# A selective scan in four layers: units of 128 channels by one state against units of 64 channels by two

## The chip, the core and the metric

The kernel runs on one core of a Trainium2 chip. Times are device microseconds (us) of that core. In the profile PE is the matrix engine (PEld its weight loads), DVE is VectorE, ACT is ScalarE, POOL is GpSimd, and SP is the engine whose queue issues all the transfers (DMAs) here. L804 is line 804 of the kernel before.

## The reference, cut to what matters

Four layers of a two-dimensional state space model (SS2D) run one after the other on an image batch of 8 x 48 x 48 with 96 channels. In each layer the input is projected to 192 inner channels and convolved to u; then, for K = 4 directions (rows, columns, and both reversed), there is a scan over the L = 2304 positions, with N = 16 states per channel:

```python
delta = jax.nn.softplus(dts + dt_projs_bias.reshape(K, Din)[None, :, :, None])
def step(h, inp):
    u, dl, Bv, Cv = inp
    dA = jnp.exp(dl[..., None] * A)
    h = h * dA + (dl * u)[..., None] * Bv[:, :, None, :]
    y = jnp.einsum('bkdn,bkn->bkd', h, Cv)
    return (h, y)
```

For each channel, state and position there is one exponential, one product with B, one step of the scan, one product with C, and a sum over the 16 states. Afterwards the directions are added, normalised, gated and projected back.

## The kernel before, in words

The image batch is taken in pairs of images. The 2 x 192 channels of a pair fill three tiles of 128 partitions: t = 0 and 1 hold the first 128 channels of each image, t = 2 the last 64 of both. For each layer, pair, tile and direction (ph for rows or columns, d for forward or reversed) the positions are cut into three chunks of 768. A unit is one chunk and one state n: 128 channels by 768 positions. Layers 0 to 2 have 3 x 4 x 12 x 3 = 432 chunks and 6912 units. Layer 3 works on short pieces at the ends of the image (the class Edge), four states to a unit.

A unit goes through the engines like this:

- SP loads the row C of state n, broadcast to 128 partitions, into a tile cb (`load`, L715), three units ahead (LOADS).
- ScalarE makes da = exp(A delta) (`exp`, L726), two or three units ahead (DECAYS).
- PE spreads the row B over 128 partitions by a product with a matrix of zeros and ones, into the PSUM tile b (`spread`, L743), one unit ahead. There are two such tiles.
- VectorE multiplies b by delta u (`scan`, L755) and scans (L759).
- GpSimd multiplies cb by the result (L768).
- PE adds cb into acc, by a product with the identity, four units later (`add_up`, L804, LAG = 4). After a chunk's sixteenth sum ScalarE copies acc into y (`collect`, L819); there is one acc, so the first sum of the next chunk (L798, which also brings in the y so far) waits for that copy.

Each fourth unit (n = 3, 7, 11, 15, `pooled`) differs in layers 0 to 2: B comes by a transfer into a tile bb (`load_b`, L687), GpSimd multiplies it by delta u (`weigh`, L698), and ScalarE's exponential goes to PSUM, into one of the two tiles b.

For the next chunk, `prepare` makes delta (c.dl) and delta u (c.du) beside the units, in two halves of 384 positions: a projection on PE (L585), softplus on ScalarE and GpSimd, its last step on VectorE (L607), a copy to c.dl on ScalarE (L609), and the product with u on VectorE (L611 or L614). The loop in `run` takes one step of it per unit. It begins at n = 0 and must be through at n = 13, when the first exponential of the next chunk is issued. Beside the units, the previous pair's epilogue and the next pair's prologue also go on in small steps.

The order of each engine is the program's order (`keep_order`), so what stands ahead in an engine's queue must be done first, its waits included. The loop issues per unit, in this order: loads, the spread, GpSimd's B, exponentials (`get_ready`), copies of the carries, the products and scan, then the sum of four units ago and one step each of `prepare` and of the side work.

Of the kernel before, what the change touches and what calls it, by code (L numbers as in the profile page):

```python
# [63 lines left out]
QUAD = 4  # L64

# [37 lines left out]
def ss2d_layers_kernel(ctx: ExitStack, tc: tile.TileContext, x_in, consts, weights, out):  # L103
# [10 lines left out]
    bbpool = ctx.enter_context(tc.tile_pool(name="bb", bufs=3))  # L114
    apool = ctx.enter_context(tc.tile_pool(name="da", bufs=5))
# [34 lines left out]
    pick = cpool.tile([NR, NS], BF16, name="pick")  # L150
    pick2 = cpool.tile([2 * NR, NS, P], BF16, name="pick2")
    sel = cpool.tile([P, 2, NS], F32, name="sel")
    for b in range(2):
        nc.vector.tensor_reduce(
            sel[:, b, :],
            ident[:, NR * b : NR * b + NR].rearrange("p (k n) -> p n k", k=PARTS),
            mybir.AxisListType.X,
            ALU.add,
        )
        nc.vector.tensor_copy(  # L160
            pick2[:, :, 64 * b : 64 * b + 64],
            sel[: 2 * NR, b, :].unsqueeze(2).to_broadcast([2 * NR, NS, 64]),
        )
    nc.vector.tensor_copy(pick, sel[:NR, 0, :])
# [21 lines left out]
    class Layer:  # L186
# [17 lines left out]
        def derive(self):  # L204
# [11 lines left out]
            nc.scalar.activation(self.a, self.a, AF.Copy, scale=-1.0)  # L216
            yield
# [335 lines left out]
    def load_dt(c):  # L553
        r = layers[c.l].rank
        c.dts = sm2.tile([64, SCAN], F32, name="dts", tag="dts")
# [6 lines left out]

    def prepare(c):
# [3 lines left out]
        c.dl = ddpool.tile([P, SCAN], F32, name="dl", tag="dl")[:, : c.m]  # L567
        c.du = ddpool.tile([P, SCAN], F32, name="du", tag="du")[:, : c.m]
# [6 lines left out]
        for z in range(0, c.m, HALF):  # L575
# [33 lines left out]
            nc.scalar.copy(c.dl[:, at], v)  # L609
            if ph == 0:  # L610
                nc.vector.tensor_mul(c.du[:, at], v, u[:, c.c0 + z : c.c0 + z + m])  # L611
            else:
                r0 = (c.c0 + z) // H
                nc.vector.tensor_mul(  # L614
                    c.du[:, at].rearrange("p (w h) -> p w h", h=H),
# [3 lines left out]
            if z + m == c.m and l == NLAYER - 1:  # L619
                c.sum_up()  # L620
            if z + m == c.m:
                yield
# [6 lines left out]
    def columns_of(l, t, ph, d, n):  # L629
        k = ph + 2 * d  # L630
        return layers[l].a[:, int(t == 2), k * NS + n : k * NS + n + 1]

    def picked(t, n):

        if t == 2:
            return 2 * NR, pick2[:, n, :]
        return NR, pick[:, n : n + 1].to_broadcast([NR, P])

# [13 lines left out]
    class Chunk:  # L652


        def __init__(self, l, p, t, ph, d, i, group, turned):
# [6 lines left out]
            self.brow = self.acc = self.dts = None  # L662
            self.cb, self.da, self.rq, self.b = {}, {}, {}, {}

        def sum_up(self):

            f = self.dl if self.d == 0 else self.dl[:, ::-1]
            nc.vector.tensor_tensor_scan(
                f, ones.to_broadcast([P, self.m]), f,
                0.0 if self.first else self.group["sum"], ALU.mult, ALU.add,  # L670
            )
            self.group["sum"] = z = capool.tile([P, 1], F32, name="sum", tag="sum")
            nc.scalar.copy(z, f[:, self.m - 1 : self.m])
# [4 lines left out]

        def load_b(self, n):
            if not self.pooled(n):  # L680
                return
            s, m, at = state[self.l, self.p], self.m, slice(self.c0, self.c0 + self.m)
            row = 2 * layers[self.l].rank + 2 * NS * self.d + n
            self.b[n] = b = bbpool.tile([P, SCAN], F32, name="bb", tag="bb")
            for z in self.batches:
                o = b[64 * z : 64 * z + 64] if self.t == 2 else b
                nc.sync.dma_start(  # L687
                    o[:, :m],
                    s["xd"][self.ph, z, row : row + 1, at].to_broadcast(
                        [64 if self.t == 2 else P, m]  # L690
                    ),
                )

        def weigh(self, n):

            if self.pooled(n):
                b = self.b[n][:, : self.m]
                nc.gpsimd.tensor_mul(b, b, self.du)  # L698

        def load(self, n):  # L700

            s, m, at = state[self.l, self.p], self.m, slice(self.c0, self.c0 + self.m)
            if n == 0:
                self.brow = rpool.tile([2 * NR, SCAN], BF16, name="brow", tag="brow")
                for j, b in enumerate(self.batches):
# [4 lines left out]
            row = 2 * layers[self.l].rank + 2 * NS * self.d + NS + n  # L710
            self.cb[n] = cb = cbpool.tile([P, SCAN], F32, name="cb", tag="cb")
            for b in self.batches:
                o = cb[64 * b : 64 * b + 64] if self.t == 2 else cb
                rows = s["xd"][self.ph, b, row : row + 1, at]
                nc.sync.dma_start(  # L715
                    o[:, :m], rows.to_broadcast([64 if self.t == 2 else P, m])
                )
# [6 lines left out]
        def exp(self, n, da):  # L724
            self.da[n] = da = da[:, : self.m]
            nc.scalar.activation(  # L726
                da, self.dl, AF.Exp, scale=columns_of(self.l, self.t, self.ph, self.d, n)
            )

        def spread(self, n):  # L730
# [9 lines left out]
            k, w = picked(self.t, n)  # L740
            self.b[n] = b = pb.tile([P, 2 * BANK], F32, name="b", tag="b")
            for z, zm in pieces(self.m):
                nc.tensor.matmul(  # L743
                    b[:, z : z + zm], w, self.brow[:k, z : z + zm], start=True, stop=True
                )

        def scan(self, n):
# [6 lines left out]
            if not self.pooled(n):  # L754
                nc.vector.tensor_mul(b, self.du, b)  # L755
# [30 lines left out]
        def add_up(self, n):  # L786
# [3 lines left out]
            elif n == 0:  # L790
# [6 lines left out]
                for a in range(2):  # L797
                    nc.tensor.matmul(  # L798
                        self.acc[:, a, : self.m // 2], w, self.y_part(z)[:, a],
                        start=True, stop=False,  # L800
                    )
            c = self.halves(self.cb.pop(n)[:, : self.m])
            for a in range(2):
# [527 lines left out]
```

## Time and profile before

The median of three runs is 21131.63 us (21129.68 to 21134.72).

| what | value |
|---|---|
| profiled execution, span | 21129.7 us |
| PE, sums (L804) | 27648 records, 10706.0 us busy |
| PE, spreads (L743) | 10368 records |
| DVE, scans (L759) | 6912, mean 1736 to 1814 ns |
| DVE, products (L755) | 5184, mean 948 ns |
| ACT, exponentials (L726) | 6912, mean 903 to 926 ns |
| POOL, products (L768) | 6912, mean 1813 ns |
| all transfers | 3832.96 MB, 61.9% of the queues' time |
| mean granted clock of PE | 0.951 |

A matrix product in 32-bit floats shows as two records. A busy engine is one that has a record running; the ends of PE's records are modelled, so a busy PE needn't be at its peak. The times of groups overlap between engines and aren't to be added up. A wait is named by the instruction that came late and by the one that released it.

### The profile page before, as it was taken

The page shows a single profiled execution, that of the slowest core. Times are in us where ns is not written, and L with a number is a line of the kernel's source. Part 1 is how long each engine was busy: PE and PEld are TensorE (multiplying, and loading weights), DVE is VectorE, ACT ScalarE, POOL GpSimd, SP SyncE. Part 2 cuts the span into 40 slices and gives each one's busy share as a digit, 9 for nine tenths or more (in the row PEclk, how much of TensorE's full clock was granted, in tenths as well). Part 3 has the DMA queues.
Part 4 walks back from the last instruction along what each step waited for, and adds up shares of the span by engine and source line. Part 5 has one row for each costly group of instructions (what it writes and reads, how often), then busy time and mean ns, then how long its engine had stood idle before and what let it go on. Part 6 is the DMA issues. An engine that isn't in the chain of part 4 may idle for free. (4 is left out here: it accounts for less than half of the span.)

```text
span 21129.7 us, 229163 instructions
## 1 busy us (share of the span) xinstructions
PE 18566.6 (88%) x64610; PEld 9118.1 (43%) x64610; DVE 18834.4 (89%) x15938; ACT 13520.6 (64%) x23969; POOL 17984.5 (85%) x11081
## 2 busy tenths in 40 slices
PE   8988998998998998998998988998998998988886
PEld 3333444443444443443443443443443443444555
DVE  6999999999999999999999999999999999997453
ACT  5555666666666665665666666665665666667776
POOL 5999898898899899898899989898999899896442
PEclk8999999999999999999999999999999999999887
DMA  4666666676676676676676666666666666674221
GB/s 137 195 193 193 188 196 194 190 196 195 190 200 195 192 201 195 190 204 191 191 204 195 191 194 195 190 197 190 191 197 193 190 196 195 189 194 123 79 74 51
DMA packets 1707632, 3832.96 MB, mean 181 GB/s; under 512 B 238448, under 2 KB 575216, under 8 KB 1693168
## 3 DMA queue, kind: packets, MB, share of 16 engines
q1 hardware_dynamic: 1706352, 3818.21, 61.9%
q8 instruction: 521, 8.54, 0.2%
q14 instruction: 759, 6.22, 0.1%
HBM read 3665.08 MB, written 152.27 MB: 181 GB/s over the span
## 5 line engine op out<-in xcount | busy, mean ns | idle before, releaser
L804 PE MATMUL acc<-cb,cst 128*128 128x384 f32 x27648 | 10706.0, 516 | 0.0
L768 POOL TENSOR_TENSOR cb<-cb,da 128x768 f32<-128x768 f32 x5184 | 9349.5, 1813 | 1393.2 <-DVE da L759 875.6
L804 PEld LDWEIGHTS acc<-cb,cst 128*128 128x128 f32 x27648 | 5003.6, 196 | 3957.4 <-issue 1498.2
L759 DVE TENSOR_TENSOR_SCAN da<-da,carry,b 128x768 f32<-128x768 f32 x3456 | 6268.3, 1814 | 220.9 <-ACT b L726 3.7
L755 DVE TENSOR_TENSOR b<-du,b 128x768 f32<-128x768 f32 x5184 | 4912.0, 948 | 685.4 <-PE b L743 678.8
L726 ACT ACTIVATE da<-dl,a 128x768 f32<-128x768 f32 x5184 | 4770.4, 926 | 95.6 <-POOL cb L768 60.4
L743 PE MATMUL b<-brow,pick 48*128 48x512 bf16 (+3 forms) x10368 | 2652.0, 337 | 1581.8 <-DVE da L759 1239.4
L726 ACT ACTIVATE b<-dl,a 128x768 f32<-128x768 f32 x1728 | 1560.3, 903 | 2960.1 <-DVE da L759 2817.4
L698 POOL TENSOR_TENSOR bb<-bb,du 128x768 f32<-128x768 f32 x1728 | 3131.3, 1812 | 183.4 <-DMA bb<-xd 142.8
L768 POOL TENSOR_TENSOR cb<-cb,bb 128x768 f32<-128x768 f32 x1728 | 3134.0, 1814 | 161.5 <-issue 56.8
L759 DVE TENSOR_TENSOR_SCAN da<-da,b 128x768 f32<-128x768 f32 x1728 | 3030.5, 1754 | 110.2 <-ACT b L726 2.4
L743 PEld LDWEIGHTS <-pick 48*128 48x128 bf16 (+1 forms) x10368 | 669.2, 97 | 4379.9 <-DVE da L759 2363.1
L759 DVE TENSOR_TENSOR_SCAN bb<-b,carry,bb 128x768 f32<-128x768 f32 x1152 | 2069.3, 1796 | 5.9 <-ACT b L726 2.2
L301 PE MATMUL ps<-pad,diag 128*128 128x480 f32 (+1 forms) x4320 | 2015.0, 565 | 15.1 <-DVE du L611 9.6
L650 ACT COPY carry<-da 128x1 f32<-128x1 f32 x3456 | 627.1, 181 | 1086.3 <-DVE da L759 1076.4
L590 ACT ACTIVATE ps<-ps,w 128x384 f32<-128x384 f32 (+1 forms) x912 | 497.1, 545 | 1027.5 <-PE ps L585 1022.9
L301 PEld LDWEIGHTS ps<-pad,diag 128*128 128x128 f32 x4320 | 804.2, 193 | 725.2 <-issue 330.3
L603 POOL TENSOR_TENSOR lg<-lg,w 128x384 f32<-128x384 f32 (+1 forms) x912 | 892.4, 978 | 195.0 <-ACT w L601 194.8
L585 PE MATMUL ps<-dts,w 6*128 6x384 f32 (+5 forms) x2432 | 821.2, 523 | 240.6 <-DVE du L611 99.9
L759 DVE TENSOR_TENSOR_SCAN bb<-b,bb 128x768 f32<-128x768 f32 x576 | 1000.1, 1736 | 16.3 <-POOL bb L698 9.8
L604 POOL TENSOR_TENSOR lg<-lg,e 128x384 f32<-128x384 f32 (+1 forms) x912 | 889.5, 975 | 71.2
L798 PE MATMUL acc<-y,cst 128*128 128x384 f32 x1008 | 619.1, 745 | 192.2 <-ACT y L819 127.2
(141 smaller groups left out, 17243.9 us busy)
## 6 DMA issues: line engine op xcount, KB each, us to landing
cb<-xd SPq DMA_DIRECT2D x4736, 384.0 KB
cb<-xd SPq DMA_DIRECT2D x4736, 192.0 KB
bb<-xd SPq DMA_DIRECT2D x1152, 384.0 KB
bb<-xd SPq DMA_DIRECT2D x1152, 192.0 KB
yd<-y SPq DMA_DIRECT2D x48, 1152.0 KB
ey<-yd SPq DMA_DIRECT2D x256, 216.0 KB
brow<-xb SPq DMA_DIRECT2D x576, 72.0 KB
ex<-xs SPq DMA_DIRECT2D x256, 108.0 KB
```

The source lines that it names most:

```text
L301: nc.tensor.matmul(ps[:, :m], ly.diag[:, int(t == 2), j, :], pad[:, r0 + dy : r0 + dy + nr, dx : dx + W], start=(j == 0), stop=(j == 8),)
L585: nc.tensor.matmul(o[:, :m], ly.dtw[q0 : q0 + r, k, chans], dts[q0 : q0 + r, at], start=True, stop=True,)
L603: nc.gpsimd.tensor_sub(lg, lg, w1)
L604: nc.gpsimd.tensor_add(lg, lg, e)
L650: nc.scalar.copy(*late_act.pop(0))
L698: nc.gpsimd.tensor_mul(b, b, self.du)
L726: nc.scalar.activation(da, self.dl, AF.Exp, scale=columns_of(self.l, self.t, self.ph, self.d, n))
L743: nc.tensor.matmul(b[:, z : z + zm], w, self.brow[:k, z : z + zm], start=True, stop=True)
L755: nc.vector.tensor_mul(b, self.du, b)
L759: nc.vector.tensor_tensor_scan(way(h), way(da), way(b), start, ALU.mult, ALU.add)
L768: nc.gpsimd.tensor_mul(c, c, h)
L804: nc.tensor.matmul(self.acc[:, a, : self.m // 2], ident, c[:, a, :], start=False, stop=(n == NS - 1 and not self.turns),)
```

## The change

A unit becomes 64 channels by two states. Unit n works on half g = n % 2 of the tile's channels, and on states n // 2 and n // 2 + 8: the first in partitions 0 to 63, the second in 64 to 127. Therefore delta and delta u have to stand in both halves of the partitions, once for each g. ScalarE copies each half to its own place, and a transfer on SP's queue, SBUF to SBUF, makes the twin (`to_twins`). The rates A are rearranged the same way (`a2`). The rows of B and C are fetched or spread per 64 partitions.

The sum over states now has to add the two halves of the partitions as well: PE multiplies by two identities of 64 stacked on each other (`twin`), which gives 64 rows of output, and it does so for both g, into the two halves of acc. Those are two tiles of 64 columns of the array. A sum takes two units at once, at odd n, and LAG is 3.

`prepare` begins one unit earlier, right after the last scan of a chunk, and what must be through at n = 13 is delta alone (`ready`); delta u may follow until the chunk ends. In the buffers, delta and delta u double, and bb goes from 3 to 2, da from 5 to 4, dts from 2 to 1. The core of the diff:

```diff
-    bbpool = ctx.enter_context(tc.tile_pool(name="bb", bufs=3))
-    apool = ctx.enter_context(tc.tile_pool(name="da", bufs=5))
+    bbpool = ctx.enter_context(tc.tile_pool(name="bb", bufs=2))
+    apool = ctx.enter_context(tc.tile_pool(name="da", bufs=4))
...
+    pick = cpool.tile([2 * NR, 2, NS], BF16, name="pick")
...
+    twin = cpool.tile([P, 64], F32, name="twin")
+    nc.vector.tensor_add(twin, ident[:, 0:64], ident[:, 64:P])
...
-        c.dts = sm2.tile([64, SCAN], F32, name="dts", tag="dts")
+        c.dts = sm1.tile([64, SCAN], F32, name="dts", tag="dts")
...
+    def to_twins(z, at):
+
+        nc.sync.dma_start(z[64:P, 0, at], z[0:64, 0, at])
+        nc.sync.dma_start(z[0:64, 1, at], z[64:P, 1, at])
+
     def prepare(c):
...
-        c.dl = ddpool.tile([P, SCAN], F32, name="dl", tag="dl")[:, : c.m]
-        c.du = ddpool.tile([P, SCAN], F32, name="du", tag="du")[:, : c.m]
+        dl = ddpool.tile([P, 2, SCAN], F32, name="dl", tag="dl")[:, :, : c.m]
+        du = ddpool.tile([P, 2, SCAN], F32, name="du", tag="du")[:, :, : c.m]
+        c.dl, c.du = ([z[:, 0], z[:, 1]] for z in (dl, du))
...
             nc.vector.scalar_tensor_tensor(v, v, 0.0, lg, ALU.max, ALU.add)
             yield
-            nc.scalar.copy(c.dl[:, at], v)
-            if ph == 0:
-                nc.vector.tensor_mul(c.du[:, at], v, u[:, c.c0 + z : c.c0 + z + m])
...
+            for g in range(2):
+                nc.scalar.copy(dl[64 * g : 64 * g + 64, g, at], v[64 * g : 64 * g + 64])
+            to_twins(dl, at)
             if z + m == c.m:
-                yield
+                if l == NLAYER - 1:
+                    c.sum_up()
+                c.ready = True
+            yield
+            times_u(v)
+            yield
+            for g in range(2):
+                nc.scalar.copy(du[64 * g : 64 * g + 64, g, at], v[64 * g : 64 * g + 64])
+            to_twins(du, at)
...
+    def spread_rows(o, rows, batches, states):
+
+        for h, (b, n) in enumerate(zip(batches, states)):
+            nc.tensor.matmul(
+                o[64 * h : 64 * h + 64], pick[:, b, n : n + 1].to_broadcast([2 * NR, 64]), rows,
+                start=True, stop=True,
+            )
...
+        def states(self, n):
+            return n // 2, n // 2 + PAIRED
+
+        def fetch(self, o, first, n):
+
+            xd = state[self.l, self.p]["xd"]
+            b = n % 2 if self.t == 2 else self.t
+            for h, i in enumerate(self.states(n)):
+                row = 2 * layers[self.l].rank + 2 * NS * self.d + first + i
+                nc.sync.dma_start(
+                    o[64 * h : 64 * h + 64, : self.m],
+                    xd[self.ph, b, row : row + 1, self.c0 : self.c0 + self.m].to_broadcast(
+                        [64, self.m]
+                    ),
+                )
...
-                da, self.dl, AF.Exp, scale=columns_of(self.l, self.t, self.ph, self.d, n)
+                da, self.dl[n % 2], AF.Exp,
+                scale=layers[self.l].a2[:, int(self.t == 2), n % 2, k, i : i + 1],
...
-                nc.vector.tensor_mul(b, self.du, b)
+                nc.vector.tensor_mul(b, self.du[n % 2], b)
...
+            if n % 2 == 0:
+                return
+            c = [self.halves(self.cb.pop(i)[:, : self.m]) for i in (n - 1, n)]
+            for a in range(2):
+                for g in range(2):
                     nc.tensor.matmul(
-                        self.acc[:, a, : self.m // 2], w, self.y_part(z)[:, a],
-                        start=True, stop=False,
+                        self.acc[64 * g : 64 * g + 64, a, : self.m // 2], twin, c[g][:, a, :],
+                        start=False, stop=(n == NS - 1 and not self.turns),
                     )
-            c = self.halves(self.cb.pop(n)[:, : self.m])
-            for a in range(2):
-                nc.tensor.matmul(
-                    self.acc[:, a, : self.m // 2], ident, c[:, a, :],
-                    start=False, stop=(n == NS - 1 and not self.turns),
-                )
...
-    LAG = 4
+    LAG = 3
...
-            if n == 0:
-                drain(coming)
...
+            if k == 0:
+                coming_to = 1
+                coming = prepare(chunks[coming_to])
             if n == max(0, per - 1 - DECAYS):
-                drain(coming)
+                while coming_to < len(chunks) and not chunks[coming_to].ready:
+                    next(coming)
...
             c.scan(n)
+            if n == per - 1:
+                drain(coming)
...
+                coming_to = chunks.index(c) + 2
+                coming = prepare(chunks[coming_to]) if coming_to < len(chunks) else iter(())
```

## The prediction

> **What bounds the kernel now.** I read the busy shares first, then VectorE's waits, then the order of time inside one chunk of 16 units.
>
> From the page, part 1:
>
> ```profile
> PE 18566.6 (88%) x64610; PEld 9118.1 (43%) x64610; DVE 18834.4 (89%) x15938; ACT 13520.6 (64%) x23969; POOL 17984.5 (85%) x11081
> ```
>
> Three engines look almost full. PE is the least so: its ends are modelled, and in the timeline four records of L804 in a row take 1.56 us and eight 2.85, so one adds 0.32. By that the 27,648 records of L804 fill about 8.9 ms, not 10.7. VectorE's rows are honest: 6912 units of a scan of 1.8 us, and 5184 products of 0.95 us, are 17.3 ms. Stretch by stretch VectorE is 93 to 95% busy from 0.5 to 19 ms (layers 0 to 2) and half idle in layer 3. So VectorE sets the time of layers 0 to 2, and a faster PE is worth only what VectorE waits for PE. The table of waits says how much (waiter, releaser: total us, times, longest):
>
> ```profile
> PE b L743 <- DVE da L759: 1239.4, 959, 5.2
> DVE b L755 <- PE b L743: 678.8, 619, 6.2
> PEld acc L798 <- ACT y L819: 241.7, 248, 4.1
> ```
>
> 679 us is the whole prize, 3.2%. The third line is one cause: the first sum of a chunk waits for the copy of the last one, and the broadcasts behind it on PE are late. The clock is another. Two stretches of 10 us (PE, PEld, DVE, ACT, POOL busy, granted clock, DMA share, GB/s):
>
> ```profile
> 5028.00:5038.00 10.00, 7.71 (x26) 3.40 (x24) 9.82 (x10) 8.62 (x21) 8.63 (x7) 1.00 0.75 216
> 5050.00:5060.00 10.00, 10.00 (x16) 4.17 (x16) 7.71 (x6) 7.48 (x11) 6.08 (x5) 0.50 0.40 111
> ```
>
> At half clock PE is full and VectorE falls to 77%.
>
> Now the end of a chunk without carries (unit 12 ends at 4950.40; the rows are the products and scans of units 13, 14, 15 and 16, then ScalarE's exponentials of 15, 17 and on):
>
> ```profile
> 4950.77 0.95 DVE L755 TENSOR_TENSOR b<-du,b 128x768 f32<-128x768 f32 x1
> 4951.75 1.81 DVE L759 TENSOR_TENSOR_SCAN da<-da,carry,b 128x768 f32<-128x768 f32 x1
> 4953.48 0.94 DVE L755 TENSOR_TENSOR b<-du,b 128x768 f32<-128x768 f32 x1
> ...
> 4956.19 1.79 DVE L759 TENSOR_TENSOR_SCAN bb<-b,carry,bb 128x768 f32<-128x768 f32 x1
> 4957.90 0.94 DVE L755 TENSOR_TENSOR b<-du,b 128x768 f32<-128x768 f32 x1
> ```
> ```profile
> 4953.66 0.91 ACT L726 ACTIVATE b<-dl,a 128x768 f32<-128x768 f32 x1 [4.43 <-DVE da L759]
> 4954.50 2.57 ACT L726 ACTIVATE da<-dl,a 128x768 f32<-128x768 f32 x3
> ```
>
> ScalarE idles at 64%, but it isn't ahead here: the exponential of unit 15 goes into the broadcast buffer that unit 13 frees, and starts 0.1 us after unit 13's scan. Whatever stands behind it in ScalarE's queue is tied to VectorE's progress.
>
> **What the Trainium skill says.** "TensorEngine Tiling (Array Packing)", Theoretical Speedup: a stationary side of at most 64 columns allows up to 2x. The trace agrees, since the epilogue has such pairs; both rows are at half clock with four records of 144 columns:
>
> ```profile
> 5047.32 1.17 PE L1018 MATMUL ps<-exn,w 96*128 96x144 f32 x4
> 5048.42 0.75 PE L1022 MATMUL ps<-exn,w 96*64 96x144 f32 x4
> ```
>
> Its Key Properties say that a change of tiling mode drains the array; in the trace L804 to L585's 64-column form takes 0.41 us instead of 0.32. "TensorE: Matmul & The Clock Gate", Part 1: an idle PE drops to half clock until it is busy again; the stretches above show it. "DMA: Bandwidth & Descriptors", Anatomy of one DMA, puts a fixed 2.0 us on a transfer (for GpSimd's queue; here SP issues).
>
> **The change, part by part.**
>
> *Sums.* Per two units four products become eight records again, but in pairs: 4 x 0.33 = 1.3 us instead of 8 x 0.32 = 2.6. That takes 3456 x 1.3 = 4.4 ms off PE; none of it is time in itself. Since LAG is 3 and sums come at even n, the turn of acc moves to n = 2 and 3, and the next broadcast behind it (unit 5's) isn't needed until two units later. I take 80% of the 679 us as gained, 560 (400 to 660 as bounds: most of these waits are behind sums, some behind side matmuls).
>
> *Broadcasts* (L743): two records become four in pairs, 96 rows for all; the same 0.33 us. The 48-row form, which drained against L804, is gone; side work at 128 columns now drains instead. Even.
>
> *VectorE.* The product with u writes PSUM instead of SBUF: 0.53 (ph 0) and 0.79 us (ph 1) as before. Nothing.
>
> *Loads.* cb and bb are two transfers of 64 rows for every unit. The third tile (t = 2) does this before (4736 of 192 KB). SP spends about 0.53 us on each against 0.32 us for one of 128 rows, so some 1.1 of a unit's 2.7 us: hidden, since cb is loaded three units ahead. The twins add 864 x 4 x 98 KB = 340 MB to 3833: 62% of the queues becomes 67%.
>
> *Copies.* Per half chunk ScalarE makes four copies of 64 rows instead of one of 128: 864 x 3 x 0.47 = 1.2 ms more, 70% busy. Hidden but for the place below. bb with 2 buffers and da with 4 instead of 3 and 5: each is released two or more units before it is wanted again; in layer 3, which waits on other work half the time, 0 (at most 40 us either way).
>
> *The twins' two round trips.* This decides. At n = 13 ScalarE gets: two copies of delta's second half, then the exponential of the next chunk's unit 0 (call it 16), which reads the half that SP's DMA copies; then carry, exponential 15, exponential 17, carry, and at n = 14 the two copies of delta u, after which SP copies again and only then VectorE can multiply for unit 16. Before, VectorE wrote delta u itself. Let R be the time from an issue on SP to the waiter's start, and zero the end of unit 12's scan.
>
> ScalarE's chain: softplus' last step on VectorE 0.54 (L607), 0.06 to wake, copy 0.47 (L609): SP issues at 1.1. Exponential 16 starts at 1.1 + R. Exponentials follow 0.84 apart (4953.66 to 4954.50), carries take 0.09: 0.93 + 0.84 + 0.93, and the copy 0.47, make 3.17. Side work between them is none in two chunks of three, 0.5 to 2 us in the rest, 0.2 on average. SP issues delta u at 4.47 + R, and it lands at 4.47 + 2R.
>
> VectorE's chain: 0.54, unit 13 2.71, the product with u 0.66, unit 14 2.71, unit 15 1.71 (starts of the rows above): ready at 8.33.
>
> So it waits 2R - 3.86 at each of 431 chunk starts. What is queued behind the two waits has more room: exponential 15 ends at 2.9 + R, and its scan starts at 6.6; SP's loads behind the twins are three units early; the next chunk's first projection on PE waits for the copies of delta u alone, about a unit. Before has no SBUF-to-SBUF transfer, so R is bounded. Below: the constants' load on the empty chip, issue at 0.74, ScalarE starts at 3.22, 2.48 us for 176 KB; a twin has 98, so 2.2 is the least I allow. Above: a small transfer in the loop,
>
> ```profile
> 4958.75 0.32 SPq L558 DMA_DIRECT2D dts<-xd  x1
> 4961.31 0.91 PE L585 MATMUL ps<-dts,w 6*128 6x384 f32 x2 [1.09 <-DMA dts<-xd]
> ```
>
> takes 2.56, and others up to 3.3, with loads queued behind them as the twins will have. I take 2.75: a wait of 1.64 us, 431 x 1.64 = 707 us. Ends: 2.2 gives 0.54 us or 233, 3.3 gives 2.74 us or 1181.
>
> *Sum.* The profiled execution took its span of 21129.7, two below the median. 21130 - 560 + 707 = 21277, and 3 for the first chunk's twins: 21280 (+0.7%).
>
> **The rivals.**
>
> *The twins are nearly covered, faster.* Same place, R smaller[...]. At R = 2.3, 0.74 us and 319 us: 21130 - 560 + 319 = 20890. It decides where 431(2R - 3.86) = 560, at R = 2.58. For it: the 2.56 above. Against it: most waits of POOL for loads of 64 rows run 3 us and more.
>
> *Half clock.* After, PE streams per four units (10.9 us) 1.0 for broadcasts, 2.7 for sums and about 2 of side work (an estimate from the records left): 52% instead of some 75. The clock will be halved far more often, and a pair of steps then holds 1.5 + 2.7 + 2 = 6.2 us on VectorE's 5.5 where side work is dense. If that brings the waits for PE back in full, the gain is gone and the twins stay: 21130 + 707 = 21840. Against it: a PE so full at half clock regains the full one.
>
> *The column tiles don't run side by side* (the change doesn't do what it says): PE keeps its load, some 100 us of gain from the new place of acc: 21740. L1022 speaks against it.
>
> **Numbers.** Forecast (R 2.65 to 3.3, slower) 0.55, its own range 21160 to 21700; nearly covered 0.25; a draw within 0.2% (about what a measurement of this kernel can tell from no change) 0.09; half clock 0.08; no overlap 0.03. Slower is 0.55 + 0.08 + 0.03 = 0.66, faster 0.25, same 0.09. The range leaves a tenth at each end: 20850 to 21720.
>
> **What would show it.** Right: VectorE's wait for PE's b under 150 us; a new wait of VectorE's product for the DMA du<-du (or for ScalarE's du), 430 times, 1 to 2.5 us each, and ScalarE's exponential waiting for dl<-dl; sums at 64 columns busy for about half of 10.7 ms at full clock; granted clock well under 0.95. Wrong: no wait at chunk starts (R was small, or ScalarE was ahead), or VectorE waiting for PE as before.

## The result, and the profile after

The changed kernel takes 23121 us (median of 4 runs, 23099 to 23151) against 21133 (21130 to 21137) for the kernel before on the same chip: 1.094 times, with a 95% interval of 1.0925 to 1.0956. It is slower, as forecast, but by 1988 us where 147 were forecast, and far outside the range. The profiled execution spans 23110.2 us, with a mean granted clock of 0.809 instead of 0.951.

The page's part 1 of the kernel after:

```profile
PE 16669.5 (72%) x77186; PEld 7088.3 (31%) x77186; DVE 18923.1 (82%) x15937; ACT 14816.1 (64%) x26555; POOL 18028.4 (78%) x11081
```

VectorE does the same work in nearly the same time as before (18923 us against 18834) and is now idle for 18% of the span. So the question is again what VectorE waits for. The table of waits of the kernel after (waiter, releaser: total us, times, longest):

```profile
ACT da L765 <- DMA dl<-dl: 1944.9, 380, 14.1
...
PE ps L602 <- ACT du L657: 1161.1, 472, 9.2
...
DVE b L795 <- PE b L668: 651.3, 644, 6.2
...
DVE bb L799 <- ACT b L765: 461.3, 216, 10.8
...
DVE b L795 <- DMA du<-du: 377.8, 198, 5.3
```

The first line is the largest new wait: the exponential of a chunk's first unit, which is L765 now, waits 5.1 us on average for the twin of delta. The second is PE's projection (L602), which waits for ScalarE's copies of delta u to give its PSUM bank back. The third answers the 678.8 us of before: VectorE waits for broadcasts as long as it did.

The end of a chunk, where unit 12's scan ends at 4884.32 in the timeline of the kernel after; VectorE's rows, then ScalarE's, then SP's:

```profile
4892.81 1.76 DVE L799 TENSOR_TENSOR_SCAN bb<-b,bb 128x768 f32<-128x768 f32 x1 [2.21 <-DMA cb<-xd]
4896.34 0.96 DVE L795 TENSOR_TENSOR b<-du,b 128x768 f32<-128x768 f32 x1 [1.77 <-PE ps L602]
```
```profile
4884.82 0.97 ACT L647 COPY dl<-ps 64x384 f32<-64x384 f32 x2 [2.91 <-DVE ps L624]
4890.90 0.94 ACT L765 ACTIVATE da<-dl,a 128x768 f32<-128x768 f32 x1 [5.12 <-DMA dl<-dl]
...
4891.83 0.90 ACT L765 ACTIVATE b<-dl,a 128x768 f32<-128x768 f32 x1
...
4893.69 0.97 ACT L657 COPY du<-ps 64x384 f32<-64x384 f32 x2
```
```profile
4877.82 1.10 SPq L725 DMA_DIRECT2D bb<-xd  x2
4879.01 2.46 SPq L725 DMA_DIRECT2D cb<-xd  x4
4881.52 1.55 SPq L750 DMA_DIRECT2D brow<-xb  x2
4883.16 1.14 SPq L725 DMA_DIRECT2D cb<-xd  x2
4885.31 0.48 SPq L576 DMA_DIRECT2D dl<-dl  x1
...
4894.19 0.48 SPq L576 DMA_DIRECT2D du<-du  x1
```

Follow the times from zero at 4884.32. SP issues delta's twin at 0.99 (forecast 1.1). Exponential 16 starts at 6.58: R is 5.59 us, where 2.75 was taken and 3.3 was the upper end. Exponential 15 stands behind it in ScalarE's queue, starts at 7.51, and so VectorE's scan of unit 15 is 2.21 us late. (The profile names DMA cb<-xd as the releaser of that scan. But the scan started 0.08 us after exponential 15 ended, and it reads what that exponential writes.) The copies of delta u follow, SP issues their twin at 9.87, and the product of unit 16 starts 2.15 us later. This second R is below the estimate. The rows of SP show what differs between the two: ahead of delta's twin ten issues went out without a pause, and ahead of delta u's none for three microseconds.

Over all 431 chunk starts of layers 0 to 2 the medians are 5.44 us from issue to exponential 16 (5th to 95th percentile 2.6 to 7.1) and 2.20 us from issue to product 16. Sorted by the number of loads that SP had issued in the 4 us before delta's twin, the first is 2.65 us with one load (17 chunk starts), 3.58 with two (59), 4.67 with three (143), 5.64 with four (114) and 6.30 with five (87).

VectorE's idle time, added up over the trace by the instruction that it ended at, in us:

```
layers 0 to 2                                before    after
ahead of the product of a chunk's unit 0         66      792
ahead of the scan of unit 15                      5      939
ahead of the products of units 9 and 10          69      448
ahead of the other products                     550      206
ahead of the other scans                        348      472
time of the three layers                      19021    20970
```

These five rows rise by 1819 of the 1949 us; layer 3 takes 25 us more. The first two, 1660 us, are the chunk's start. The third is the projection. The fourth is the only gain.

### The profile page after: what moved, and what is told of

The parts are those of the page before. It is cut to its first block, busy times and chain, and to the rows that moved or that the text cites. A ratio compares the mean times of both kernels' runs of the same rounds, so it can differ in the third digit from the quotient of the medians.

```text
span 23110.2 us, 285479 instructions
## 1 busy us (share of the span) xinstructions
PE 16669.5 (72%) x77186; PEld 7088.3 (31%) x77186; DVE 18923.1 (82%) x15937; ACT 14816.1 (64%) x26555; POOL 18028.4 (78%) x11081
## 5 line engine op out<-in xcount | busy, mean ns | idle before, releaser
L849 PE MATMUL acc<-cb,twin 128*64 128x384 f32 x27648 | 6739.1, 599 | 55.8 <-POOL cb L808 55.0
L765 ACT ACTIVATE da<-dl,a 128x768 f32<-128x768 f32 x5184 | 4808.6, 928 | 2957.0 <-DMA dl<-dl 1944.9
L668 PE MATMUL b<-brow,pick 96*64 96x256 bf16 (+2 forms) x22272 | 3414.1, 389 | 3826.7 <-DVE da L799 2894.3
L668 PEld LDWEIGHTS <-pick 96*64 96x64 bf16 x22272 | 1126.0, 122 | 7406.7 <-DVE da L799 4801.1
L849 PEld LDWEIGHTS acc<-cb,twin 128*64 128x64 f32 x27648 | 2443.4, 167 | 2772.4 <-issue 2105.5
L602 PE MATMUL ps<-dts,w 6*128 6x384 f32 (+5 forms) x2432 | 1259.7, 769 | 1567.8 <-ACT du L657 1161.1
L312 PE MATMUL ps<-pad,diag 128*128 128x480 f32 (+1 forms) x4320 | 2331.1, 640 | 36.5 <-ACT du L657 19.6
L765 ACT ACTIVATE b<-dl,a 128x768 f32<-128x768 f32 x1728 | 1555.0, 900 | 1181.4 <-DVE da L799 1124.1
L647 ACT COPY dl<-ps 64x384 f32<-64x384 f32 x1728 | 816.3, 472 | 1568.1 <-DVE ps L624 1546.7
L312 PEld LDWEIGHTS ps<-pad,diag 128*128 128x128 f32 x4320 | 734.2, 203 | 1170.6 <-issue 1044.2
L602 PEld LDWEIGHTS ps<-dts,w 6*128 6x128 f32 (+3 forms) x2432 | 343.4, 222 | 1970.2 <-ACT du L657 1474.5
```

What stands on the lines that cost most here:

```text
L312: nc.tensor.matmul(ps[:, :m], ly.diag[:, int(t == 2), j, :], pad[:, r0 + dy : r0 + dy + nr, dx : dx + W], start=(j == 0), stop=(j == 8),)
L602: nc.tensor.matmul(o[:, :m], ly.dtw[q0 : q0 + r, k, chans], dts[q0 : q0 + r, at], start=True, stop=True,)
L647: nc.scalar.copy(dl[64 * g : 64 * g + 64, g, at], v[64 * g : 64 * g + 64])
L668: nc.tensor.matmul(o[64 * h : 64 * h + 64], pick[:, b, n : n + 1].to_broadcast([2 * NR, 64]), rows, start=True, stop=True,)
L765: nc.scalar.activation(da, self.dl[n % 2], AF.Exp, scale=layers[self.l].a2[:, int(self.t == 2), n % 2, k, i : i + 1],)
L849: nc.tensor.matmul(self.acc[64 * g : 64 * g + 64, a, : self.m // 2], twin, c[g][:, a, :], start=False, stop=(n == NS - 1 and not self.turns),)
```

## The experiments

Three theories on the late twin were put side by side. It stands behind loads, in SP's queue or in the DMA engines that serve it; ScalarE has too much to do at that place; or the transfer from SBUF to SBUF is slow in itself. A second question was where the gain of the lighter PE had gone.

### Delta's twins without a transfer

ScalarE writes both rows of delta itself, from PSUM, and delta u's twins stay transfers.

```diff
-                nc.scalar.copy(dl[64 * g : 64 * g + 64, g, at], v[64 * g : 64 * g + 64])
-            to_twins(dl, at)
+                for h in range(2):
+                    nc.scalar.copy(dl[64 * h : 64 * h + 64, g, at], v[64 * g : 64 * g + 64])
```

> Delta's two twins are written by ScalarE (four copies of 64 partitions from PSUM instead of two copies and two transfers); delta u's twins stay transfers. In the trace after, a chunk start costs VectorE 2.2 us at the scan of unit 15 and 1.8 us at the product of unit 16, some 1.7 ms in all. Theory A (delta's twin is late because it is queued behind loads on the same queue: 5.4 us from issue to waiter): the exponential of unit 16 starts 2.3 us after unit 12's scan instead of 6.6, the wait at the scan of unit 15 goes (939 us to under 100), and with delta u's transfer at 2.2 us as now the wait at the product goes too: 23120 - 1650 = about 21500. If delta u's transfer takes over the place behind the loads (5.4 us), some 2.5 us per chunk stay: about 22500. Theory B (ScalarE has too much to do at the chunk's end, whoever makes the twin): two more copies there, no gain or a loss, 23100 or more.

Measured: 22359 us, 1.0579 (1.0561 to 1.0596). Exponential 16 starts at 2.46 after unit 12's scan instead of 6.5, and VectorE's idle time ahead of the scan of unit 15 falls from 939 to 17 us. So two more copies of 0.47 us on ScalarE are no burden there, and the wait was for the transfer. But the median from the issue of delta u's twin to product 16 rises from 2.20 to 4.22 us. The twin is issued 3.4 us earlier (at 6.5 instead of 9.9) and so falls among the loads: product 16 waits 1196 us in all instead of 792. The time that went was not simply the twin's.

### The loads behind delta's twin

The loads that SP issues in the step before delta's twin are issued one step later.

```diff
-            early(LOADS, "load")
+            late = 0 < k < len(todo) and todo[k][0][0] not in short and todo[k][2] in (13, 14)
+            if late and todo[k][2] == 14 and k + LOADS - 1 < len(todo):
+                todo[k + LOADS - 1][1].load(todo[k + LOADS - 1][2])
+            if not late or todo[k][2] == 14:
+                early(LOADS, "load")
```

> Only the order on SP's queue is changed: the load of the next chunk's first unit (two B rows and two of C) is issued one step later, behind delta's second twin, so that nothing stands ahead of it. Theory A: the exponential of unit 16 waits 2.2 to 3.5 us for the twin instead of 5.4, the waits at the chunk start fall by about 2 to 3 us of 4: 22000 to 22300. Theory C (a transfer from SBUF to SBUF of this size is slow by itself or starved by the loads issued after it): no change, 23000 to 23200.

Measured: 24106 us, 1.1403 (1.1384 to 1.1422), outside both expectations. R of delta's twin falls from 5.44 to 2.21 us, with nothing changed about the transfer or ScalarE: so it is neither slow in itself nor ScalarE's load. The loads that were put back now stand ahead of delta u's twin, whose R rises from 2.20 to 5.89. VectorE's largest wait in this run (377.8 us in the kernel after):

```profile
DVE b L795 <- DMA du<-du: 2561.7, 392, 9.8
```

The whole bill moved from one twin to the other and grew. Part of the growth is not R: delta u's twin itself goes out late. In one chunk start (zero at 5296.26; SP's rows, then ScalarE's):

```profile
5297.25 0.48 SPq L576 DMA_DIRECT2D dl<-dl  x1
...
5298.42 1.59 SPq L750 DMA_DIRECT2D brow<-xb  x2
5300.11 2.42 SPq L725 DMA_DIRECT2D cb<-xd  x4
5302.62 1.18 SPq L725 DMA_DIRECT2D bb<-xd  x2
5303.90 1.18 SPq L725 DMA_DIRECT2D cb<-xd  x2
5305.18 0.54 SPq L576 DMA_DIRECT2D du<-du  x1
```
```profile
5302.68 0.97 ACT L657 COPY du<-ps 64x384 f32<-64x384 f32 x2
```

The first copy of delta u is done at 5303.2, but SP is still issuing the ten loads ahead of the twin, 0.5 to 0.8 us each, and gets to it two microseconds later. The median of this delay is 2.45 us here and 0.03 in the kernel after. With its mean, 2.21, and the mean values of R, 2.50 and 5.85, the wait is 2.21 + 2.50 + 5.85 - 3.86 = 6.70 us per chunk, 2888 us in all. VectorE's idle time ahead of products 16 and scans 15 is 2889 us above that of the kernel before.

### The twins on a queue of their own

This asks whether it is the order of SP's queue or the work of the DMA engines. ScalarE issues the twins, on a queue that carries nothing else in the loop.

```diff
-        nc.sync.dma_start(z[64:P, 0, at], z[0:64, 0, at])
-        nc.sync.dma_start(z[0:64, 1, at], z[64:P, 1, at])
+        nc.scalar.dma_start(z[64:P, 0, at], z[0:64, 0, at])
+        nc.scalar.dma_start(z[0:64, 1, at], z[64:P, 1, at])
```

> The changed kernel, with both twins' transfers issued by ScalarE instead of SP, on a queue that holds nothing else in the loop. If the twin of delta is slow because loads stand ahead of it in SP's queue, it lands in about 2.2 to 2.7 us instead of 5.4 and exponential 16 starts about 3 us earlier: 21500 to 22200, less what issuing costs ScalarE (two issues per half chunk). If it is slow because the DMA engines themselves are busy with the loads, the queue changes little: 22900 to 23400.

Measured: 24582 us, 1.1628 (1.1608 to 1.1647): neither expectation. On a queue of their own the twins' packets can be told from all others. The table gives the median time from the issue of a pair (two transfers of 98 KB, issued 0.56 us apart) to the last packet of both, by the number of loads that SP had issued in the 4 us before:

```
loads in the 4 us before   delta's twin (times)   delta u's twin (times)
0                          2.38 us (527)          -
1                          2.38 us (149)          3.72 us (16)
2                          2.38 us (95)           3.92 us (39)
3                          2.50 us (59)           3.54 us (41)
4                          2.99 us (21)           3.66 us (83)
5                          -                      5.14 us (272)
6                          -                      5.78 us (374)
```

Both columns are the same pair of transfers on the same queue. While such a pair was under way, the loads on SP's queue moved nothing in the first row and 0.95 MB in the last (medians); over all pairs, the time and these bytes go together with a correlation of 0.94. So a queue of its own does not protect a twin: what else the DMA engines have in flight decides. (Delta u's column is slower at the same count, so the count of loads is a rough measure of it.) The median from the issue of delta's twin to exponential 16 is 2.15 us in this run, about as the first expectation had it; but since SP's loads now mostly stand still before that twin, this doesn't tell the order from the engines, and delta u's column does. Of the first theory's two forms the second holds for a twin that has been issued. The first has a part of its own, the late issue that loads_behind_twin shows. That the kernel became slower still has another cause. SP's waits in this run and in the kernel after:

```profile
SPq L725 <- DMA dl<-dl: 4692.9, 920, 9.3
SPq L725 <- DMA du<-du: 3250.7, 966, 9.5
```
```profile
SPq L725 <- PE acc L849: 3533.2, 1632, 11.5
SPq L576 <- ACT du L657: 1954.0, 775, 8.5
```

SP's loads now wait until the twins have landed, for 7.9 ms in all, and PE then waits for late rows of B (3308 us of PE's idle time end at brow<-xb). Why the loads wait for transfers of another queue, whether for a semaphore that both share or otherwise, wasn't tried apart. In the kernel after, the fourth line shows a smaller wait of the same kind: SP stands for 1954 us at the issue of delta u's twins until ScalarE has copied, with its loads queued behind. What this costs VectorE wasn't measured.

### The product with u a step earlier

delta_by_act, and VectorE multiplies by u in the same step, into an SBUF buffer; ScalarE copies delta u from it one step earlier than before. Only delta u's twins are transfers.

```diff
+            w2 = sm1.tile([P, HALF], F32, name="w2", tag="w1")[:, :m]
+            times_u(w2)
...
-            times_u(v)
-            yield
...
-                nc.scalar.copy(du[64 * g : 64 * g + 64, g, at], v[64 * g : 64 * g + 64])
+                nc.scalar.copy(du[64 * g : 64 * g + 64, g, at], w2[64 * g : 64 * g + 64])
```

> As delta_by_act, and VectorE's product with u goes to a buffer in SBUF in the same step as the copies of delta; so it no longer overwrites PSUM, the bank is free without waiting for ScalarE's copies of delta u, and prepare is one step shorter per half. PE's wait for the copies of delta u (1161 us, and VectorE's waits for b at n = 9 and 10, 448 us) should go along with the chunk start's: theory A 20700 to 21000, below the kernel before if the lighter PE gives its 400 us. Theory B: 22500 or more.

Measured: 21125 us, 0.9992 (0.9983 to 1.0001), a little above the range expected: the whole loss is gone. The twin is issued at 1.4 after unit 12's scan and has six microseconds. VectorE's waits from 500 to 19300 us, first of the kernel before, then of this one:

```profile
DVE b L755 <- PE b L743: 672.2, 611, 6.2
```
```profile
DVE b L795 <- PE b L668: 271.1, 299, 5.9
DVE b L795 <- DMA du<-du: 202.5, 67, 6.7
...
DVE bb L799 <- ACT b L765: 49.2, 34, 2.4
DVE eyc L1080 <- ACT ps L270: 38.2, 26, 4.5
```

Two things are seen. The prize is real, 400 us of waits for broadcasts, though the clock is 0.841 and PE at half clock for 32% of layers 0 to 2 (7.5% before). It lies at units 6 and 8, where VectorE waited 307 and 103 us for broadcasts in the kernel before and doesn't wait now; units 1 and 2 lose, 106 us before and 184 now. The change also moved the turn of acc, behind which unit 6's broadcast stood, so this prize belongs to the lighter sums and the new place of acc together, and no run tells them apart. And the wait ahead of units 9 and 10, 448 us after and 390 in delta_by_act, is 47: it came from the projection (L602), which waits on PE for the copies of delta u while broadcasts stand behind it. With the copies a step earlier the wait of L602 for them is gone from the table, where it had 1161 us after. What eats most of the prize is 203 us for the twin in 67 chunks, some 110 us in small waits for ScalarE (two of them are shown; ScalarE is 74% busy instead of 64%), and 42 us in layer 3.

### No twin by a transfer

product_by_sbuf, with delta u's twins copied by ScalarE too.

```diff
-                nc.scalar.copy(du[64 * g : 64 * g + 64, g, at], w2[64 * g : 64 * g + 64])
-            to_twins(du, at)
+                for h in range(2):
+                    nc.scalar.copy(du[64 * h : 64 * h + 64, g, at], w2[64 * g : 64 * g + 64])
```

> As product_by_sbuf, and the twins of delta u are also made by ScalarE's copies (four of 64 rows instead of two, read from the SBUF buffer of the product), so that no twin goes by a transfer. If the 234 us that the product of a chunk's first unit still waits in product_by_sbuf (0.54 us per chunk) are the twin's transfer of 6.3 us, they go, against 864 x 2 x 0.47 us = 0.8 ms more on ScalarE, 78% busy: 20850 to 21000. If ScalarE is by then the engine that VectorE waits for, the copies come back as waits of the scans for exponentials: 21100 to 21500.

Measured: 21150 us, 1.0005 (0.9996 to 1.0014): no change against the kernel before, and none that can be told from product_by_sbuf. No product waits for a twin any more, but VectorE's waits for broadcasts rise from 271 to 383 us and those for ScalarE's side work too (eyc L1080 and L1058: 38 and 2 us before this step, 73 and 32 with it). ScalarE is 78% busy. The 203 us went, and other waits of about the same sum came.

### The loads behind delta u's twin

product_by_sbuf with loads held back by a step, as in loads_behind_twin. The first form held back the wrong step's:

> product_by_sbuf with the next chunk's loads of the step before delta u's twin issued one step later, behind the twin (the edit of loads_behind_twin). So far a twin took 2.2 us where no loads had been issued in the 3 us before it and 5 to 6.5 us where four to six had, on SP's queue and on ScalarE's alike. So R for delta u falls from 6.3 to about 2.2 to 2.5 us, it lands near 4 us and no first product waits for it: the 203 us of those waits go, 20900 to 21000. If the loads that come one step later are then late for VectorE's scans or PE's broadcasts, as they may be with less slack, these waits take the place: 21100 to 21300.

Measured: 21134 us, 0.9996 (0.9987 to 1.0004). The twin is issued a step later than delta's, so the loads that were held back still went out ahead of it: the last of them starts at a median of 0.6 us after zero, as without the edit, and the twin at 1.4. The second form moves the edit on by a step:

```diff
-            late = 0 < k < len(todo) and todo[k][0][0] not in short and todo[k][2] in (13, 14)
+            late = 0 < k < len(todo) and todo[k][0][0] not in short and todo[k][2] in (14, 15)
```

> product_by_sbuf with the loads of the step in which delta u's twin is issued put behind it (product_by_sbuf_late_loads held back the loads of the step before and gave them out still ahead of the twin, so R stayed at 6.4 us and the time at 21134). If loads issued shortly ahead make the twin slow, R for delta u falls to 2.2 to 3 us, the 203 us of first products that wait for it go and half of the 131 us of PE's waits at the start of a chunk with them: 20880 to 21000. If they have no such effect, R stays above 5 and the time at 21130.

Measured: 21055 us, 0.9962 (0.9948 to 0.9976), between the two expectations and 0.4% faster than the kernel before. VectorE's waits from 500 to 19300 us:

```profile
DVE b L795 <- PE b L668: 262.0, 275, 5.1
DVE b L795 <- DMA du<-du: 126.9, 41, 5.6
```

The waits for the twin fall by 76 us of the 203, and the time by about 63 by the two ratios. The number that the expectation gave for R stayed at 6.5, but it was the wrong number: it ended at the start of product 16, which in most chunks isn't waiting. The waits that remain are chunks in which the twin is issued late, at a median of 4.0 us after zero instead of 1.3 in the others. In one of them:

```profile
1540.33 1.05 ACT L657 COPY du<-w 64x384 f32<-64x384 f32 x2
1545.90 0.54 SPq L576 DMA_DIRECT2D du<-du  x1
1552.54 0.96 DVE L795 TENSOR_TENSOR b<-du,b 128x768 f32<-128x768 f32 x1 [5.56 <-DMA du<-du]
```

The copy was done at 1540.9, but SP issued twelve loads of bb, cb, brow and raw in the ten microseconds before the twin, and came to it five microseconds late.

### Half of the sums, three quarters of them

The second question, on the kernel before: what does PE's work cost? Here the sums of even states are left out, and nothing else is changed.

```diff
+            if n % 2 == 0:
+                return
             c = self.halves(self.cb.pop(n)[:, : self.m])
```

> The kernel before, with the sums of the even states left out (their products with C are made, but not added; PE has half the work in L804, as with two column tiles). What a lighter PE is worth in the old layout: by the prediction's term 400 to 560 us of the 679 that VectorE waits for PE, so 20570 to 20730. If half clock takes the gain back: 20900 to 21100.

Measured: 21389 us, 1.0117 (1.01 to 1.0133). The sums take 7.1 ms of PE's busy time instead of 10.7, and the kernel is 256 us slower. In the second run only the second half of the columns of even states' sums is left out:

```diff
-            for a in range(2):
+            for a in range(1 + n % 2):
```

> The kernel before with the second half (384 of 768 columns) of the sums of even states left out: three quarters of the sums' products, in the same order. All of them took 21133, half of them 21389. If PE's clock is the cause, the time lies between, 21180 to 21330, with a clock between 0.81 and 0.95, and what a broadcast takes lies between too. If leaving out work had another effect that is not one of the clock, such as a change in what the sums wait for, there is no reason for an order: it may be at 21133 or below, with VectorE waiting less for PE as PE has less to do.

Measured: 21346 us, 1.0095 (1.008 to 1.011), a little above the upper end of the forecast. PE's groups by shape in the kernel before, with three quarters of the sums and with half (busy us, mean ns of one):

```profile
L743 PE MATMUL b<-brow,pick 48*128 48x512 bf16 x3456 | 1369.8, 396 | 777.0 <-DVE da L759 727.9 <-DVE bb L759 21.9 <-DMA cb<-xd 14.0
```
```profile
L743 PE MATMUL b<-brow,pick 48*128 48x512 bf16 x3456 | 1447.1, 419 | 1449.6 <-DVE da L759 1392.5 <-DMA cb<-xd 24.0 <-DVE bb L759 18.6
```
```profile
L743 PE MATMUL b<-brow,pick 48*128 48x512 bf16 x3456 | 1574.9, 457 | 2019.6 <-DVE da L759 1983.3 <-DMA cb<-xd 19.7 <-DMA brow<-xb 8.1
```

The order of PE's instructions is the same in all three. The less it sums, the longer the same broadcast takes: 396, 419, 457 ns; the granted clock is 0.951, 0.895, 0.814, and layers 0 to 2 are at half clock for 7.5, 20 and 38% of their time. VectorE waits for broadcasts 679, 895 and 909 us. So taking work off PE slows the work that is left. The traces can be sorted by the clock that was granted when an instruction started. A record of the form shown takes a median of 387 ns at full clock and 604 or 605 at half clock in all three kernels; of the 3456 records, 161, 505 and 1116 start at half clock. So the longer mean is the larger share of half clock and nothing else. And VectorE's waits for broadcasts that end at half clock are 145, 472 and 486 us, those at full clock 533, 423 and 423: the rise is all at half clock. That the clock is the cause of this rise, and not a companion of it, is argued, not shown: the next runs tried to show it.

### Work that nobody reads

Each gives PE products whose results nobody reads, to hold the clock. In half_the_sums, behind each broadcast:

```diff
+            for _ in range(2):
+                nc.tensor.matmul(b[:, 768:1024], ident, cst[:, 0:256], start=True, stop=True)
```

> The kernel before without the sums of even states, as half_the_sums, with two products of 256 columns more behind each broadcast, into columns of b that nobody reads: about 1.3 us per four units given back of the 2.6 taken away... (each 256 columns at 0.21 us at full clock: 0.43 us per unit, 1.7 per four units). It computes only half the sums. If half_the_sums is slower than before (21389 against 21133) because PE, with less to do, loses its full clock, the clock rises from 0.81 towards 0.92 or more and the time falls to 21000 to 21150. If it is slower for another reason (the order of sums and broadcasts), it stays at 21390 or rises.

Measured: 22565 us, 1.0674 (1.0656 to 1.0692). The clock did rise, to 0.928, but the time rose too. The waits say why:

```profile
DVE b L757 <- PE b L747: 1963.0, 1715, 4.8
```

The filler writes the broadcast's own buffer, so VectorE's product waits for the filler. Each product of float data is two records (20736 for 10368), so it also took twice what the expectation counted, 6.1 ms busy. The run doesn't answer its question. What it does show is how bare this place is: about 1.2 us of PE behind each of 5184 broadcasts cost 1176 us. The same with 64-column pairs in the changed kernel without twin transfers:

> As no_twin_dma, and PE has four half-height products of 256 columns more per broadcast of a unit's b, in pairs, into columns of b that nobody reads: work that no one waits for, to keep PE busy. If PE's half clock is what makes VectorE wait for broadcasts and for sums (the waits rose by 260 us where half the sums were left out and nothing else was changed), the clock goes from 0.84 back above 0.9 and the time falls by 50 to 250 us against no_twin_dma. If the waits come from the order of PE's queue, PE's extra 0.22 us per unit makes it the same or up to 300 us slower.

Measured: 21547 us, 1.019 (1.0173 to 1.0207), clock 0.889 instead of 0.844, and the same flaw (828 us of waits for the filler). The last one puts four pairs of 128 columns behind each sum, into spare columns of acc, where VectorE waits for them only as far as they delay PE:

```diff
+            for a in range(4 * (n < NS - 1)):
+                for g in range(2):
+                    nc.tensor.matmul(
+                        self.acc[64 * g : 64 * g + 64, a % 2, 384:512], twin, cst[:, 0:128],
+                        start=False, stop=False,
+                    )
```

> product_by_sbuf_late_loads, and PE has four pairs of 128-column products more behind each sum, into columns of acc that nobody reads, 0.44 us per two units at full clock: work that neither VectorE nor ScalarE waits for directly, unlike the filler behind the broadcasts. If half clock makes what is left of VectorE's waits for PE (271 us), the clock rises from 0.84 to 0.88 or more and the time falls by 30 to 200 us. If PE's queue itself is what VectorE waits for, it is 0 to 300 us slower.

Measured: 21181 us, 1.002 (1.0013 to 1.0028), against 21134 without the filler. The clock rose from 0.842 to 0.904 and the share of half clock fell from 32 to 18%, but VectorE's waits for broadcasts rose from 250 to 354 us. So with the sums in pairs the half clock is not worth buying off: the work that holds the clock costs more of PE's time than the clock gives back.

## Why the prediction was wrong

**What held.** VectorE sets the time, its own work is unchanged, and the twins' two round trips decide. ScalarE's chain was right to a tenth: the twin's issue at 0.99 (1.1), exponentials 0.83 apart (0.84), and 3.29 us from exponential 16 to the issue of delta u's twin (3.37). The formula was right as well. With the two mean values of R that the trace shows, 5.18 and 2.42 us, the wait, both of them less 3.86, becomes 3.74 us per chunk, 431 of them 1612 us; the idle time at the chunk's start rose by 1660. The sums do run side by side (eight records in 1.51 us at full clock instead of 2.85), so that rival falls.

**The step that failed: R, from "a small transfer in the loop".** It was sized at 2.75 us, with an upper end of 3.3, from transfers that had loads behind them. Loads behind do no harm: in loads_behind_twin R of delta's twin was 2.2 with them there. Loads ahead do. The trace of the kernel before had one example, in the load that the prediction chose (SP's rows, then PE's):

```profile
188.90 0.85 SPq L706 DMA_DIRECT2D brow<-xb  x1
189.79 2.70 SPq L715 DMA_DIRECT2D cb<-xd  x5
192.53 0.80 SPq L558 DMA_DIRECT2D dts<-xd  x1
```
```profile
199.17 1.61 PE L585 MATMUL ps<-dts,w 6*128 6x384 f32 x2 [4.55 <-DMA dts<-xd]
```

With six loads in the 4 us ahead of it R is 6.64 us. In the loop of layers 0 to 2, all 21 waits of PE for this load had one or two ahead, and R was 2.5 to 3.6. In the 4 us before the place of delta's twin SP issues a median of three, in the kernel before as in the kernel after, and up to seven. So R was measured in a quieter place than the one it was used for. The term of 707 us measured 1660. The mechanism was right and its size was off by more than twice.

**"What is queued behind the two waits has more room": wrong for two of the three.** Exponential 15 was given room until 6.6, which holds for R up to 3.7; with 5.2 its scan is late at 361 chunk starts, 939 us. This is inside the 1660, since the wait only begins earlier. What SP's standing at the twin's issue cost, with loads behind it, isn't known. The third is PE's projection:

**The projection "waits for the copies of delta u alone, about a unit": priced at nothing, cost 379 us.** It blocks the broadcasts of units 9 and 10 behind it. product_by_sbuf, which makes the copies a step earlier, has 47 us there instead of 448.

**The gain of 560 us: there, but smaller.** Without the projection's block VectorE's waits for broadcasts fell by 400 us (672 to 271), the lower end of the bounds given, and not to the 150 us or less that was to show it; in the kernel after, the products other than those of units 0, 9 and 10 gained 344. The total of 651 us in the waits of after looks as if the *half clock* rival had come true (its words: the waits come back in full), and the clock did fall as it said. But at a clock of 0.841 product_by_sbuf has less than half of those waits. By place, 307 of the 679 us before stood at unit 6 and 67 at units 9 and 10; after, 2 and 442. So most of the 651 us is the projection's and not the half clock's, although half_the_sums shows that in the kernel before a lighter PE is a slower one.

**Readings that don't hold.** The two stretches do not show that an idle PE loses its clock and a busy one regains it. What the trace shows is this: the half clock of the second stretch is granted from 5046.84 to 5060.50, after 2.60 us without a product (5042.67 to 5045.27); and PE was busy all through these 13.65 us and still kept the half clock. So "a PE so full at half clock regains the full one" had no support there. Of the sums, 3456 x 1.3 is 4.5 ms, and R = 3.3 gives 21751 with the gain of 560, above the range's end of 21700. Neither matters for the outcome.

**The sum, with measured terms.** 1660 for the chunk's start, 379 for the projection, 124 for other scans and 25 for layer 3, less 344: 1844 of the 1980 us between the two spans. Of the rest, 89 us is VectorE's longer busy time; what remains isn't traced one by one. No case held the result, because all of them took the same R of 2.2 to 3.3.

## What to carry to other kernels

Before you put a new transfer on the path that sets the end, count the bytes issued in the few microseconds ahead of it, and price the wait at that backlog, not at what a transfer takes in a quiet place; count also the issues that stand ahead of it in its own queue. Another queue did not help here. Let a producer run a step earlier before anything else: here that, with its product in SBUF, took back 1235 us, and the place of the loads then gave some 60 more. And read a wait total by place before you take it for the same wait: 679 and 651 us for the same pair of lines had different causes.

## What was not expected of the hardware

Two 98 KB transfers within SBUF, issued 0.56 us apart, have landed 2.38 us after the first issue where no load was issued in the 4 us before, and after 5.8 us with six, even on a queue that carries nothing else. And PE's granted clock fell when it had less to do, from 0.951 to 0.895 and 0.814: with a quarter of the sums left out the same broadcast took 6% longer, with half of them 15%, and the kernel became slower by 0.95 and 1.2%.
